# Four conv layers on one core: another order of work in the tap stages, and the gate's chunks spread into them

## The chip, the cores and the metric

The kernel runs on one core of one Trainium2 chip. The metric is the device time of one execution in microseconds (us). Three executions of the kernel before took 1805.18, 1809.2 and 1817.68 us; their median, 1809.2 us, is the time that the change is held against.

## The reference, cut to what matters

The input `x` is (4, 256, 56, 56) in fp32: four images of 256 channels. Four layers follow one another, each with a group norm `_gn` (32 groups) ahead of it and its result added to its input:

```python
# layers 0 and 2: a 7x7 "involution": the taps differ at every pixel, and 16 channels share them
h    = reduce_w @ x            # 256 -> 64 channels (layer 2: then batch norm and relu)
kern = span_w @ h + span_b     # 49 taps for each of 16 groups, at each pixel
out  = sum over the 49 taps of kern * shifted x      # layer 2: then batch norm and relu
# layer 1: two 3x3 convolutions with batch norms and relus
# layer 3: a gate by Fourier transforms
cf = sigmoid(fft2(x).real.mean over pixels @ W.T + b)   # a number for each channel
sf = fft2(x.mean over channels).real                    # a number for each pixel
out = x * cf + x * sf
```

In each layer `x = x + layer(_gn(x))`. The mean over pixels of the transform's real part is the first pixel of `x`, so `cf` needs one small matrix product.

## The kernel before, in words

**Tiling and stages.** `involution_layer` (L280) is called for layer 0 and for layer 2; a convolution layer lies between. It works through eight units, (image b, channel block cb of 128 channels), cb=0 and then cb=1 of each image. A unit has two stages. In its *tap stage*, `tap_matrices` (L569) runs over 32 groups n: TensorE computes the taps of one group (L580) into a pair of PSUM banks, of which there are four pairs, and the pair is evicted with the bias added into the tile `kt`, by ScalarE (six ACTIVATEs, L591) where n % 3 is 0, and by VectorE (one TENSOR_TENSOR, L598) else. In its *column stage*, seven strips of eight pixel columns (tx 0 to 6) are done one after another by `apply`: TensorE multiplies windows of the image `xw` with `kt` (L622), ScalarE and VectorE scale, fold and add the result to the image block `xs` (L635 to L649), and `next_windows` makes the `xw` of a later strip: transposes on TensorE, a copy on ScalarE, and four transfers on SyncE's queue that shift rows (L414, L416).

**What sets the order.** It is written out by hand. `in_order` (L228) keeps every engine's instructions in the order of the program, so an instruction that waits holds all that stand behind it on its engine. Other work is cut into steps (Python generators): `place(hooks, steps, (2, 6, ...))` puts one step each behind those groups n of the tap stage, and the lists `early[tx]` and `late[tx]` put steps before or behind a strip of the column stage.

**Steps in layer 2's hooks.** Layer 3's gate is fused into layer 2. When a unit's image block is done, the next unit's tap stage takes its norm for layer 3: `norm_of(3, ...)`, made of `norm_steps` (L199): a mean over channels by TensorE (L207), differences on VectorE (L215), a second mean (L218), then 1/sqrt(variance), whose power is the GpSimd instruction L139 (hook 12), and the shift on VectorE, L222 (hook 13). In the second and third unit a second norm runs in the tap stage too, that of the last image for layer 2. `channel_mean` (L677) takes the mean over channels on TensorE (L702), and `gate_factors` (L720) loads W (`w3_sb`, SyncE), computes `cf` (L732, L739) and the transforms that give `sf`; this is once per image, in the tap stage of the next image's cb=0. An image's block of 1568 KB is loaded at hook 26 or 21.

**The gate.** For all images but the last, the gate is applied chunk by chunk (`gate_chunk`, L777), on GpSimd alone: 14 chunks per image, seven groups of eight rows by two channel blocks, chunk k being rows k // 2 and channel block k % 2. Each has two steps. `next_load` (every second time with a load of sfb, the row group's `sf` for all partitions, L783) loads the chunk `gx` (L786) into one of three buffers; `next_gate` computes (L789, L794, L795, L796) and stores it (L797). GpSimd starts these transfers itself. They stand in cb=0's column stage (tx 2 to 6), in cb=1's tap stage (hooks 16, 22, 28) and in cb=1's column stage (tx 0 to 5). In that last stage `bottleneck` (L421) makes the next image's `hp`: GpSimd clears a part (L432) at tx 0, ScalarE writes the rest (L478).

The last image's gate is done at the end by other code on more engines, from the last norm on (its power is L139 too).

Of the kernel before, what the change touches and what calls it, by code (L numbers as in the profile page):

```python
# [16 lines left out]
P = 128  # L17
# [54 lines left out]
def net_kernel(  # L72
# [207 lines left out]
    def involution_layer(layer, xin, xout, red, span, sb, xs_of, ahead=None, pending=None):  # L280

        with ExitStack() as es:
# [23 lines left out]
            if layer == 0:  # L306
                load(0, 0, (2, 2, 2, 1))
                load(0, 1, (2, 2, 2, 1))

                nc.scalar.copy(norm_sb[:, 3, B - 1, 1, :], mhalf)  # L310

            red_sb = wpool.tile([P, NB, 2, R], F32, name="red_sb")

# [255 lines left out]
            def tap_matrices(b, cb, hooks):  # L569

                hp = h_of[b]
                kt = big.tile([Q, GB, TP // PB, NT, PB], F32, name="kt")
                for n in range(GB // 2 * TP // PB):
                    gp, pb = divmod(n, TP // PB)
                    ps = two_banks()
                    for k in range(PB):
                        py, px = divmod(pb * PB + k, TX)
                        z0 = ZF - py * QX - px
                        for i in range(2):
                            nc.tensor.matmul(  # L580
                                ps[:Q, i, k * NT : (k + 1) * NT],
                                z_sb[i * R : (i + 1) * R, cb * GB // 2 + gp, z0 : z0 + Q],
                                hp[i * R : (i + 1) * R, py, px].rearrange("p a t -> p (a t)"),
                                start=True,
                                stop=True,
                            )
                    g0, p0 = 2 * gp, pb * PB
                    if n % 3 == 0:
                        for i in range(2):
                            for k in range(PB):  # L590
                                nc.scalar.activation(  # L591
                                    kt[:, g0 + i, pb, :, k],
                                    ps[:Q, i, k * NT : (k + 1) * NT],
                                    AF.Identity,
                                    bias=zb_sb[:, cb * GB + g0 + i, p0 + k : p0 + k + 1],
                                )
                    else:
                        nc.vector.tensor_tensor(  # L598
                            kt[:, g0 : g0 + 2, pb],
                            ps[:Q, :, : PB * NT].rearrange("q i (k t) -> q i t k", k=PB),  # L600
                            zb_sb[:, cb * GB + g0 : cb * GB + g0 + 2, p0 : p0 + PB]
                            .unsqueeze(2)
                            .to_broadcast([Q, 2, NT, PB]),
                            ALU.add,
                        )
                    for h in hooks.get(n, ()):
                        h()
                return kt
# [68 lines left out]
            def channel_mean(b, cb):  # L677
# [39 lines left out]
                nc.sync.dma_start(m2_of[cb], m_dram[b][cb].rearrange("j (r w) -> (j r) w", w=W))  # L717
                yield

            def gate_factors(b):  # L720


                w3_sb = [dead(b, 1, 4 * CR * W + ci * C, C) for ci in range(NB)]
                for ci in range(NB):
                    nc.sync.dma_start(w3_sb[ci], w3[ci * P : (ci + 1) * P])
                cf = small.tile([P, NB], F32, name="cf")
                cf_of[b] = cf
                yield
                for co in range(NB):
                    ps = one_bank()  # L730
                    for ci in range(NB):
                        nc.tensor.matmul(  # L732
                            ps[:, 0:1],
                            w3_sb[ci][:, co * P : (co + 1) * P],
                            first_of[b][:, ci : ci + 1],
                            start=(ci == 0),
                            stop=(ci == NB - 1),
                        )
                    nc.scalar.activation(  # L739
                        cf[:, co : co + 1], ps[:, 0:1], AF.Sigmoid, bias=cp[:, co, L3_B : L3_B + 1]  # L740
                    )
                yield

                ps = one_bank()
                for i in range(2):
                    at = slice(i * R, i * R + W)
                    for cb in range(NB):
                        nc.tensor.matmul(
                            ps[at, :H],
                            m2_of[cb],  # L750
                            sin_sb if i else cs2_sb[:H],
                            start=(cb == 0),
                            stop=(cb == NB - 1),
                        )
                yield
                for i in range(2):
                    at = slice(i * R, i * R + W)
                    nc.vector.tensor_copy(half[at], ps[at, :H])
                yield

                ps = one_bank()
                nc.tensor.matmul(ps[:H, :W], half, cs2_sb, start=True, stop=True)
                scale = small.tile([P, NB], F32, name="gscale")
                bias = small.tile([P, NB], F32, name="gbias")
                nc.vector.tensor_mul(scale, cf, norms[3][b][0])
                nc.vector.tensor_scalar_add(scale, scale, 1.0)
                nc.vector.tensor_mul(bias, cf, norms[3][b][1])
                gate_of[b] = scale, bias
                yield
                sf = small.tile([H, W], F32, name="sf", bufs=1)  # L770
                nc.vector.tensor_copy(sf, ps[:H, :W])
                nc.sync.dma_start(sf_dram[b].rearrange("j (r w) -> (j r) w", w=W), sf)
                yield

            sf_of, gate_of = {}, {}

            def gate_chunk(b, j, cb):  # L777

                rstd, shift = norms[3][b]
                at = slice(j * CR * W, (j + 1) * CR * W)  # L780
                if cb == 0:
                    sf_of[b] = work.tile([P, CR * W], F32, name="sfb", bufs=2)
                    nc.gpsimd.dma_start(sf_of[b], sf_dram[b][j : j + 1].to_broadcast([P, CR * W]))  # L783
                sf = sf_of[b]
                xs = gx_tile()
                nc.gpsimd.dma_start(xs, xout[b][cb][:, at])  # L786
                yield
                xn = work.tile([P, CR * W], F32, name="gn", bufs=1)
                nc.gpsimd.tensor_scalar(  # L789
                    xn, xs, rstd[:, cb : cb + 1], shift[:, cb : cb + 1], ALU.mult, ALU.add  # L790
                )

                scale, bias = (t[:, cb : cb + 1] for t in gate_of[b])
                nc.gpsimd.tensor_scalar(xs, xs, scale, bias, ALU.mult, ALU.add)  # L794
                nc.gpsimd.tensor_tensor(xn, xn, sf, ALU.mult)  # L795
                nc.gpsimd.tensor_tensor(xs, xs, xn, ALU.add)  # L796
                nc.gpsimd.dma_start(ov[b, cb][:, at], xs)  # L797
                yield

# [193 lines left out]
            for u, (b, cb) in enumerate(units):  # L993
                hooks = hooks0 if u == 0 else {}
                if prev is not None:
# [2 lines left out]
                    place(hooks, norm_of(layer + 1, pb, pc, st), (2, 6, 7, 11, 12, 13))  # L998
                    if layer == 2 and u < 3:
                        g = norm_of(2, B - 1, u - 1, pending[1][u - 1])  # L1000
                        place(hooks, g, (19, 20, 22, 23, 25, 26))
                    if layer == 2:
                        place(hooks, channel_mean(pb, pc), (13, 17))
                        if pc == 1:
                            place(hooks, gate_factors(pb), (17, 24, 27, 28, 30, 31))
                        elif pb == B - 1:
                            factors = gate_factors(pb)
                            place(hooks, factors, (20,))
                            hooks.setdefault(21, []).append(lambda pb=pb: last_dft(pb))
                            hooks.setdefault(22, []).append(last_ones)  # L1010
                            place(hooks, first_half(pb), (28, 29))
                    if layer == 2 and cb == 1 and b > 0:
                        for n in (16, 22, 28):
                            hooks.setdefault(n, []).extend((next_gate, next_load))
                if b + 1 < B:
                    n = 16 if layer == 0 else (26, 21)[cb]
                    hooks.setdefault(n, []).append(load_step(b + 1, cb))
# [42 lines left out]
                        early[6].append(step(g))  # L1060
                if layer == 2 and b > 0:
                    if cb == 0:
                        chunks.extend(gate_chunk(b - 1, j, c) for j in range(NCHUNK) for c in range(NB))
                        late[1] += [next_load, next_load]
                    for tx in range(2, NTX) if cb == 0 else range(NTX - 1):
                        late[tx] += [next_gate, next_load]
                if last_image and cb == 0:
                    for tx in range(6):
                        late[tx] += [step(g2)] * 3
# [652 lines left out]
```

## Time and profile before

| | us |
|---|---|
| median of three executions | 1809.2 |
| the profiled execution, of which all durations here come | 1812.46 |
| its span, first to last instruction | 1810.7 |
| layer 0 | 38 to 476 |
| convolution layer | 510 to 1240 |
| layer 2 with the gate | 1240 to 1811 |
| a tap stage, layer 0 | 24.8 to 28.2 each |
| a tap stage, layer 2 | 28.7 to 36.1 each |
| a column stage, layer 2 | 28.3 to 36.2 each |
| idle of TensorE in one stage, layer 2 | up to 5.4 |

The granted TensorE clock was 0.979 of full speed. In the profile's lines PE is TensorE's matmul, PEld its weight load, DVE VectorE, ACT ScalarE, POOL GpSimd and SP SyncE; L12 is line 12 of the kernel before. A row `PE ps L580 <- ACT kt L591: 5.8, 15, 0.9` says that TensorE's instructions of L580 waited 5.8 us in all, 15 times, 0.9 at the longest, for ScalarE's writes of `kt`, the eviction that frees a PSUM pair. A timeline's line has the start in us from the span's start, the duration, engine, line, operation, tile written and tiles read, and in brackets the wait before it with what ended it.

### The profile page before, as it was taken

How to read it: one execution, taken by the hardware profiler on the slowest of the kernel's cores; microseconds unless marked ns; L12 is line 12 of the kernel's file. 1: busy time of each engine (PE TensorE's matmuls, PEld its weight loads, DVE VectorE, ACT ScalarE, POOL GpSimd, SP SyncE). 2: the span in 40 equal slices, each digit the busy share in tenths (PEclk: the TensorE clock that was granted, in tenths of full speed). 3: DMA queues.
4: the chain of work that ended last, by engine and by line, in shares of the span. 5: the costliest groups of instructions: out<-in, count | busy, mean ns of one | idle time of the engine just before them, and what ended most of it. 6: DMA issues, size and time to landing. Idle time of an engine off the chain costs nothing.

```text
span 1810.7 us, 55835 instructions
## 1 busy us (share of the span) xinstructions
PE 1720.8 (95%) x24034; PEld 1514.9 (84%) x24034; DVE 1375.4 (76%) x2729; ACT 842.2 (47%) x1981; POOL 430.0 (24%) x626
## 2 busy tenths in 40 slices
PE   7999999999989999999999999997999999899988
PEld 6998989889878988998899889985988887887876
DVE  3787777776689988898889888875777677677775
ACT  3566556555532322322232222113767567577564
POOL 2333433245210000000000000000000374563572
PEclk9999999999989999999999999998999999999997
DMA  2545534454651201120121111031534566665653
GB/s 85 158 154 165 164 119 143 159 159 116 209 174 49 69 26 63 63 70 30 59 73 59 41 60 34 34 135 49 161 132 149 168 218 188 202 210 168 169 156 127
DMA packets 66004, 215.77 MB, mean 119 GB/s; under 512 B 13237, under 2 KB 20926, under 8 KB 62046
## 3 DMA queue, kind: packets, MB, share of 16 engines
q1 hardware_dynamic: 48718, 145.24, 25.7%
q0 software_dynamic: 14688, 64.78, 11.3%
q8 instruction: 190, 3.11, 0.7%
q10 hardware_dynamic: 2352, 2.18, 0.4%
q14 instruction: 56, 0.46, 0.1%
HBM read 76.30 MB, written 49.15 MB: 69 GB/s over the span
## 4 chain that ended last, share of the span: by engine, by line
PE 76%; DVE 9%; ACT 6%; DMA 4%; issue 2%; POOL 2%; SPq 1%; ACTq 0%; POOLq 0%; DVEq 0%
PE mm L1493 19%; PE ps L580 18%; PE ps L622 14%; PE mm L1411 10%; PE mm L1382 5%; PE ps L396 5%; DMA xw<-xw 4%; ACT kt L591 3%; PE ps L459 2%; DVE un L642 1%; DVE kt L598 1%; ACT xw L408 1%; ACT hp L478 1%; SPq L414 1%; DVE res L1486 1%
## 5 line engine op out<-in xcount | busy, mean ns | idle before, releaser
L580 PE MATMUL ps<-hp,z_sb 64*126 64x133 f32 x6144 | 392.1, 281 | 16.2 <-ACT kt L591 7.0
L622 PE MATMUL ps<-kt,xw 126*32 126x48 f32 (+1 forms) x12544 | 379.0, 236 | 24.1 <-DMA xw<-xw 12.1
L622 PEld LDWEIGHTS ps<-kt,xw 126*32 126x32 f32 (+1 forms) x12544 | 341.9, 122 | 68.2 <-issue 46.3
L580 PEld LDWEIGHTS ps<-hp,z_sb 64*126 64x126 f32 x6144 | 369.1, 187 | 34.6 <-ACT kt L591 12.7
L598 DVE TENSOR_TENSOR kt<-ps,zb_sb 126x798 f32<-126x798 f32 x336 | 319.8, 981 | 90.1 <-PE ps L580 89.5
L1493 PE MATMUL mm<-v,u_sb 128*128 128x280 f32 (+1 forms) x1728 | 385.0, 385 | 3.4 <-DVE v L1318 3.4
L1493 PEld LDWEIGHTS mm<-v,u_sb 128*128 128x128 f32 x1728 | 327.9, 190 | 57.5 <-DVE v L1318 3.8
L591 ACT ACTIVATE kt<-ps,zb_sb 126x133 f32<-126x133 f32 x1056 | 306.9, 442 | 96.2 <-PE ps L580 95.6
L1411 PE MATMUL mm<-v,u_sb 128*128 128x252 f32 (+1 forms) x936 | 212.3, 388 | 3.4 <-DVE v L1302 3.4
L1411 PEld LDWEIGHTS mm<-v,u_sb 128*128 128x128 f32 x936 | 178.3, 192 | 33.8 <-issue 3.5
L1530 POOL DMA_DIRECT2D x<-xs x24 | 13.1, 546 | 683.2 <-DVE xs L1529 427.4
L642 DVE SCALAR_TENSOR_TENSOR un<-ps,s,un 128x240 f32<-128x240 f32 x224 | 102.5, 457 | 85.7 <-ACT un L637 81.5
L642 DVE SCALAR_TENSOR_TENSOR un<-ps,par_sb,un 128x240 f32<-128x240 f32 x224 | 98.3, 457 | 87.1 <-ACT un L635 82.8
L1478 ACT ACTIVATE res<-xs,shift,norm_sb 128x1120 f32<-128x1120 f32 (+1 forms) x24 | 30.2, 1259 | 236.3 <-DVE xs L1529 107.3
L408 ACT COPY xw<-ps 126x896 f32<-126x896 f32 x112 | 101.4, 906 | 47.9 <-PE ps L396 37.7
L647 POOL TENSOR_TENSOR xs<-un,xs 128x240 f32<-128x240 f32 x112 | 72.3, 664 | 192.4 <-DVE un L642 192.3
L396 PE MATMUL ps<-ident_sb,strip_sb 128*126 128x128 f32 x784 | 111.7, 283 | 6.1 <-POOL strip_sb L381 5.8
L635 ACT ACTIVATE un<-ps,par_sb 128x240 f32<-128x240 f32 x112 | 50.1, 448 | 115.7 <-PE ps L622 113.4
L1382 PE MATMUL mm<-xs,u_sb 128*128 128x126 f32 (+1 forms) x792 | 98.6, 277 | 1.3 <-DVE xs L1345 0.9
L396 PEld LDWEIGHTS ps<-ident_sb,strip_sb 128*126 128x126 f32 x784 | 84.9, 142 | 17.0 <-POOL strip_sb L381 6.9
L637 ACT ACTIVATE un<-ps,bn_t,s 128x240 f32<-128x240 f32 x112 | 60.0, 538 | 83.3 <-PE ps L622 72.1
L1382 PEld LDWEIGHTS mm<-xs,u_sb 128*128 128x128 f32 x792 | 94.5, 191 | 2.4 <-issue 1.0
(254 smaller groups left out, 1925.8 us busy)
## 6 DMA issues: line engine op xcount, KB each, us to landing
xw<-xw SPq DMA_DIRECT2D x168, 252.0 KB
xw<-xw SPq DMA_DIRECT2D x224, 126.0 KB
xw<-xw POOLq DMA_DIRECT2D x56, 252.0 KB, 4.7
xs<-x SPq DMA_DIRECT2D x24, 560.0 KB
x<-xs POOLq DMA_DIRECT2D x8, 1568.0 KB, 8.2
xs<-x SPq DMA_DIRECT2D x8, 1568.0 KB
xs<-in_x_dram SPq DMA_DIRECT2D x6, 1568.0 KB
x<-xs SPq DMA_DIRECT2D x6, 1568.0 KB
```

Of the source, the lines that this page charges most:

```text
L396: nc.tensor.transpose(ps[:Q, k * P : (k + 1) * P], flat[:, k * Q : (k + 1) * Q], ident_sb)
L408: nc.scalar.copy(xw[:, :NSB, :], ps[:Q, : NSB * P].rearrange("q (n c) -> q n c", n=NSB))
L580: nc.tensor.matmul(ps[:Q, i, k * NT : (k + 1) * NT], z_sb[i * R : (i + 1) * R, cb * GB // 2 + gp, z0 : z0 + Q], hp[i * R : (i + 1) * R, py ...
L591: nc.scalar.activation(kt[:, g0 + i, pb, :, k], ps[:Q, i, k * NT : (k + 1) * NT], AF.Identity, bias=zb_sb[:, cb * GB + g0 + i, p0 + k : p0 ...
L598: nc.vector.tensor_tensor(kt[:, g0 : g0 + 2, pb], ps[:Q, :, : PB * NT].rearrange("q i (k t) -> q i t k", k=PB), zb_sb[:, cb * GB + g0 : cb ...
L622: nc.tensor.matmul(v[m * j : m * j + m, i, :, k * TP : (k + 1) * TP], xw[:, window(ty), m * j : m * j + m], kt[:, ng * j : ng * j + ng, :, ...
L637: nc.scalar.activation(part, o[0], AF.Identity, bias=bn["t4"][:, cb : cb + 1], scale=bn["s4"][ng][:, 0, cb : cb + 1])
L642: nc.vector.scalar_tensor_tensor(part, o[e], s, part, ALU.mult, ALU.add)
L647: nc.gpsimd.tensor_tensor(dst, u, dst, ALU.add)
L1382: nc.tensor.matmul(ps[:, co * m : (co + 1) * m], u[ci][:, co * P : (co + 1) * P], v2[:, e, : n // 2, ci * WT : (ci + 1) * WT], start=(ci = ...
L1411: nc.tensor.matmul(ps, u1_sb[:, ci, dy, k, co * P : (co + 1) * P], v[:, k, dy * NB + ci : (dy + n - 1) * NB + ci + 1 : NB, :], start=(j == 0),
L1493: nc.tensor.matmul(ps, u2_sb[:, ci, dy, k, co * P : (co + 1) * P], v[:, k, dy * NB + ci : (dy + n - 1) * NB + ci + 1 : NB, :], start=(j == 0),
```

## The change

In words, in the order of the diff:

- The first copy on ScalarE, which fills a value of the table of norms, is an activation with the function Sigmoid.
- ScalarE evicts the groups with n % 3 equal to 2, so 10 of 32 in place of 11; the first two and the last two groups are VectorE's. This holds for both involution layers.
- `w3_sb` goes into buffers of sfb for all images but the last, and its load is issued at hook 8 in place of 17.
- The gate's two numbers per channel are others: cf + 1/rstd, and −shift/rstd. A chunk is computed as gn = x·rstd + shift, then (sf + cf + 1/rstd)·gn − shift/rstd, which equals x + (cf + sf)·gn: three TENSOR_SCALAR and one TENSOR_TENSOR in place of two and two.
- sfb's first two loads stand at cb=0's tx 0; each other one is issued in a gate of cb=1's chunks, before that gate's store, two row groups ahead.
- The two first chunks of gx are loaded in cb=0's tap stage, at hooks 18 and 20. From then on each place has a load and then a gate, in place of a gate and then a load.
- The places of gates: cb=0's columns tx 1, 2, 4, 5; cb=1's tap stage, hooks 14, 18, 22, 26, 30; cb=1's columns tx 0 to 4.
- The second norm's steps stand at hooks 15, 19, 20, 24, 25, 26 in place of 19, 20, 22, 23, 25, 26.

```diff
-                nc.scalar.copy(norm_sb[:, 3, B - 1, 1, :], mhalf)
+                nc.scalar.activation(norm_sb[:, 3, B - 1, 1, :], mhalf, AF.Sigmoid)
...
-                    if n % 3 == 0:
+                    if n % 3 == 2:
...
+            def new_sf():
+                return work.tile([P, CR * W], F32, name="sfb", bufs=2)
+
             def gate_factors(b):
-                w3_sb = [dead(b, 1, 4 * CR * W + ci * C, C) for ci in range(NB)]
+                w3_sb = [new_sf()[:, :C] if b < B - 1 else dead(b, 1, 4 * CR * W + ci * C, C) for ci in range(NB)]
...
-                nc.vector.tensor_mul(scale, cf, norms[3][b][0])
-                nc.vector.tensor_scalar_add(scale, scale, 1.0)
-                nc.vector.tensor_mul(bias, cf, norms[3][b][1])
-                gate_of[b] = scale, bias
+                rstd, shift = norms[3][b]
+                nc.vector.reciprocal(back, rstd)
+                nc.vector.tensor_add(cfx, cf, back)
+                nc.vector.scalar_tensor_tensor(back, shift, -1.0, back, ALU.mult, ALU.mult)
+                gate_of[b] = cfx, back
...
+            def load_sf(b, j):
+                sf_of[b, j] = new_sf()
+                nc.gpsimd.dma_start(sf_of[b, j], sf_dram[b][j : j + 1].to_broadcast([P, CR * W]))
+
             def gate_chunk(b, j, cb):
-                if cb == 0:
-                    sf_of[b] = work.tile([P, CR * W], F32, name="sfb", bufs=2)
-                    nc.gpsimd.dma_start(sf_of[b], sf_dram[b][j : j + 1].to_broadcast([P, CR * W]))
-                sf = sf_of[b]
                 xs = gx_tile()
                 nc.gpsimd.dma_start(xs, xout[b][cb][:, at])
                 yield
...
-                nc.gpsimd.tensor_scalar(xs, xs, scale, bias, ALU.mult, ALU.add)
-                nc.gpsimd.tensor_tensor(xn, xn, sf, ALU.mult)
-                nc.gpsimd.tensor_tensor(xs, xs, xn, ALU.add)
+                nc.gpsimd.tensor_scalar(xs, sf_of[b, j], 1.0, cfx, ALU.mult, ALU.add)
+                nc.gpsimd.tensor_tensor(xs, xs, xn, ALU.mult)
+                nc.gpsimd.tensor_scalar(xs, xs, 1.0, back, ALU.mult, ALU.add)
+                if cb == 1 and j + 2 < NCHUNK:
+                    load_sf(b, j + 2)
                 nc.gpsimd.dma_start(ov[b, cb][:, at], xs)
...
-                        place(hooks, g, (19, 20, 22, 23, 25, 26))
+                        place(hooks, g, (15, 19, 20, 24, 25, 26))
...
-                            place(hooks, gate_factors(pb), (17, 24, 27, 28, 30, 31))
+                            place(hooks, gate_factors(pb), (8, 24, 27, 28, 30, 31))
+                            chunks.extend(gate_chunk(pb, j, c) for j in range(NCHUNK) for c in range(NB))
+                            for n in (18, 20):
+                                hooks.setdefault(n, []).append(next_load)
...
-                        for n in (16, 22, 28):
-                            hooks.setdefault(n, []).extend((next_gate, next_load))
+                        for n in (14, 18, 22, 26, 30):
+                            hooks.setdefault(n, []).extend((next_load, next_gate))
...
                     if cb == 0:
-                        chunks.extend(gate_chunk(b - 1, j, c) for j in range(NCHUNK) for c in range(NB))
-                        late[1] += [next_load, next_load]
-                    for tx in range(2, NTX) if cb == 0 else range(NTX - 1):
-                        late[tx] += [next_gate, next_load]
+                        late[0] += [lambda b=b, j=j: load_sf(b - 1, j) for j in range(2)]
+                    for tx in (1, 2, 4, 5) if cb == 0 else range(NTX - 2):
+                        late[tx] += [next_load, next_gate]
```

More of the change, by code (lines that the diff above doesn't have):

```diff
@@ L762, in gate_factors @@
                 nc.tensor.matmul(ps[:H, :W], half, cs2_sb, start=True, stop=True)
-                scale = small.tile([P, NB], F32, name="gscale")
-                bias = small.tile([P, NB], F32, name="gbias")
-                nc.vector.tensor_mul(scale, cf, norms[3][b][0])
-                nc.vector.tensor_scalar_add(scale, scale, 1.0)
-                nc.vector.tensor_mul(bias, cf, norms[3][b][1])
-                gate_of[b] = scale, bias
+                cfx = small.tile([P, NB], F32, name="gscale")
+                back = small.tile([P, NB], F32, name="gbias")
+                rstd, shift = norms[3][b]
[3 more added lines that the diff above has]
+                gate_of[b] = cfx, back
                 yield
@@ L791, in gate_chunk @@
                 )
[L793 to L796, printed above, removed]
+                cfx, back = (t[:, cb : cb + 1] for t in gate_of[b])
+                nc.gpsimd.tensor_scalar(xs, sf_of[b, j], 1.0, cfx, ALU.mult, ALU.add)
[3 more added lines that the diff above has]
+                    load_sf(b, j + 2)
                 nc.gpsimd.dma_start(ov[b, cb][:, at], xs)
```

## The prediction

> **What bounds the kernel now.** I read the engines' totals, then each engine's waits in the second involution layer (1130 to 1811 us, where most of the diff lies), then GpSimd's timeline and its transfers.
>
> ```profile
> PE 1720.8 (95%) x24034; PEld 1514.9 (84%) x24034; DVE 1375.4 (76%) x2729; ACT 842.2 (47%) x1981; POOL 430.0 (24%) x626
> ```
>
> TensorE has work for 95% of the span, so only about 90 us of idle can be won, and anything that holds it up is paid in full. Its waits by releaser (total us, count, longest), and below them GpSimd's:
>
> ```profile
> PE ps L622 <- DMA xw<-xw: 10.6, 10, 3.8
> PE ps L580 <- ACT kt L591: 5.8, 15, 0.9
> PE ps L702 <- DVE kt L598: 2.8, 3, 1.0
> PE ps L218 <- DVE d L215: 2.3, 2, 1.1
> PE ps L207 <- DVE mv L204: 1.9, 2, 0.9
> PE ps L732 <- ACT kt L591: 1.8, 1, 1.8
> ```
> ```profile
> POOL norm_sb L139 <- DVE norm_sb L138: 202.6, 10, 84.4
> POOL gn L789 <- DMA gx<-x: 18.1, 16, 3.9
> POOL gx L786 <- DMA out_dram<-gx: 6.4, 6, 2.2
> ```
>
> TensorE's waits are many and small; five of these six rows are touched. GpSimd waits most for the norm's power (L139): it comes there early. For a finished store (last row) it waits only 6.4 us, since a chunk's buffer is one of three and was stored a whole gate earlier. GpSimd's timeline (start, duration, wait before it in brackets) shows a gate, and one of those waits:
>
> ```profile
> 1443.37 0.71 POOL L789 TENSOR_SCALAR gn<-gx,norm_sb 128x448 f32<-128x448 f32 x1 [0.34 <-DMA gx<-x]
> 1444.18 0.71 POOL L794 TENSOR_SCALAR gx<-gx,gscale,gbias 128x448 f32<-128x448 f32 x1
> 1444.86 1.14 POOL L795 TENSOR_TENSOR gn<-gn,sfb 128x448 f32<-128x448 f32 x1
> 1446.08 1.14 POOL L796 TENSOR_TENSOR gx<-gx,gn 128x448 f32<-128x448 f32 x1
> 1447.52 0.59 POOL L797 DMA_DIRECT2D out_dram<-gx  x1 [0.30 <-POOL gx L796]
> 1448.11 0.55 POOL L783 DMA_DIRECT2D sfb<-sf  x1
> 1448.65 0.55 POOL L786 DMA_DIRECT2D gx<-x  x1
> ...
> 1482.71 0.55 POOL L786 DMA_DIRECT2D gx<-x  x1 [2.23 <-DMA out_dram<-gx]
> 1483.25 0.17 POOL L432 MEMSET hp<- 128x56 f32 x1
> ```
>
> The stores' line answers how long one takes from issue to landing:
>
> ```profile
> L797 POOL DMA_DIRECT2D out_dram<-gx x42: 592/592/619, 1435.9 to 1780.4; - x42
> DMA to landing us min/median/max: 2.3/4.7/8.4
> ```
>
> **What the Trainium skill says.** (1) "DMA: Bandwidth & Descriptors", "Anatomy of one DMA — SWDGE (gpsimd) path": a transfer started by GpSimd has a fixed part of about 2.0 us besides its bytes. The trace agrees: a 224 KB store never lands in under 2.3 us. (2) The same page, "Issuing engines are not separate DMA queues": all starters' transfers "interleave with each other". The trace agrees: stores land in 2.3 us in quiet stretches, 3.3 to 3.9 in lightly loaded columns, 7 to 8 beside a 1568 KB image. (3) "SBUF — State Buffer", "Who interferes with whom": VectorE's second port pair is GpSimd's, under an exclusive lock. The trace agrees in part: VectorE's L649 grows from 0.41 us to 0.78 to 1.07 beside gates, while the kt eviction L598, which reads PSUM, keeps 0.98.
>
> **The change, part by part.**
>
> *Gates, order and buffers.* A step is now load, gate in place of gate, load. So the load of chunk k+2 comes before gate k, and its buffer, of three, is that of chunk k−1, whose store is the instruction just before on GpSimd. Every such load therefore waits a store's whole landing, L. Queued behind it on GpSimd are the gate, then the norm's power L139 (behind it VectorE's shift L222, then kt evictions in program order, then TensorE), and the memset L432 (ACT's L478 waits for it).
>
> One gate costs GpSimd, without waits: 4.15 us from L789's start to the store's issue (1447.52 − 1443.37). The changed arithmetic has three TENSOR_SCALAR and one TENSOR_TENSOR in place of two and two: −(1.14 − 0.71) = −0.43, so 3.72. With a load at 0.57 and half an sfb load (0.55/2 = 0.27), the pitch is 4.56 + L, against 5.65 to 5.9 measured now.
>
> Between the power in a cb=1 tap stage and that in the next cb=0 tap stage lie 10 gates, 8 loads of which 7 wait, 3 sfb loads, 3 last store issues and the memset: 37.2 + 4.6 + 1.65 + 1.8 + 0.2 = 45.4, plus 7L. These powers stand 65.4 us apart in the first image (1463.97 to 1529.34) and 64.9 in the second. GpSimd keeps up while L is below (65.4 − 45.4)/7 = 2.9, or 2.8. The third image's next power is the tail's, which is already close:
>
> ```profile
> 1785.61 0.57 POOL L139 TENSOR_TENSOR norm_sb<-norm_sb,mhalf 128x1 f32<-128x1 f32 x1 [4.63 <-DVE norm_sb L138]
> ```
>
> It comes 57.5 us after the one at 1728.15. There 45.2 + 7L must fit into 57.5, plus 2.2 of TensorE work that runs behind it anyway: L below 2.1.
>
> What L will be, no row shows: loads no longer overlap the stores, but the column stages' xw transfers and the images stay. The bounds are 2.3 (the fastest store) and 4.9 (the mean of 42). I take 4.0, between the lightly loaded columns and the median, and 3.6 for the last image, which has no image load beside it. Then 45.4 + 28 = 73.4: the powers come **8.0** and **8.5** late, and the tail's 45.2 + 25.2 − 57.5 − 2.2 = **10.7**. Sum **+27.2**. At 2.3 it is 0 + 0 + 1.6; at 4.9, 14.3 + 14.8 + 19.8 = 49. The memset, behind gates 4 to 8, comes at 23.4 + 4L = 39 after the power; ACT's first L478 ran 31.8 after it. That is a delay of the same 8 us, not a second one. The four gates in cb=0 columns end some 4 us before the power; nothing is lost there. The cheaper arithmetic is hidden as long as GpSimd keeps up, and is inside the 3.72 otherwise.
>
> *Second norm's hooks* (units 1 and 2). The groups between its steps grow, so L207 (0.94), L218 (1.14) and the L580 after each (0.48, 0.86) no longer wait, in either unit: the rows sum to 4.2 for the first two over two units; with L580, 4.2 + 2 × 1.34 = 6.9. I take **−5.0** (bounds −4.2 and −6.9).
>
> *w3's load* at hook 8 in place of 17, into sfb's buffers: the L732 waits (1.8 in the row, 0.93 before another releaser) go: **−2.8**. On SyncE it now stands behind the previous image's last gate; next in that queue are transfers of hooks 17 and later, so nothing is late. VectorE's three small operations stay three: 0.
>
> *Two gx loads of each image leave the cb=0 columns for hooks 18 and 20, and two gates leave columns* (5, 3 and 6 gates in cb=0 columns, cb=1 taps and cb=1 columns become 4, 5 and 5). xw's waits there were 1.07 + 1.38, 3.77 and 0.42 + 1.73 = 8.4; the transfers that remain still share the engines, so I take half, **−4** (bounds 0 and −8.4).
>
> *n % 3 == 2.* ACT has 10 groups of 1.75 us in place of 11, VectorE 22 of 0.98 in place of 21. Two VectorE groups now start and end each stage; the column stage waits for the last of them. I take 0.4 in three gate units and 0.1 in 13 others: 1.2 + 1.3. Group 7, which carries a norm step, waits for VectorE's group 4, 0.17 in four stages of the first layer: 0.7. In the second layer the start's wait, which looks like this,
>
> ```profile
> 1321.60 2.32 PE L580 MATMUL ps<-hp,z_sb 64*126 64x133 f32 x36 [0.64 <-ACT kt L591]
> ```
>
> goes, and about as much appears at group 7. Sum **+3.2** (bounds −5.8, if nothing replaces that row, and +8).
>
> *Sigmoid at the start.* One table load of 1.28 us goes at 1411.39, where ACT then sat idle till 1415.57: 0 (bounds 0 and −1.3).
>
> *Sum.* 27.2 − 5.0 − 2.8 − 4 + 3.2 = **+18.6**. The profiled execution took 1812.46 us (span 1810.7, 1.76 around it), so 1831 for it; it lies 3.3 above the shown runs' median of 1809.2, and the forecast in terms of that is **1828**.
>
> **Rivals.** *A, the forecast:* GpSimd's landings set powers and tail, L from 3.3 to 4.7: slope 7 us per image and us of L, 1814 to 1842; 0.56. For it: the buffer's arithmetic, and a median landing of 4.7. Against: the longest landings stood beside transfers that now move. *B, on the other side:* with gx's load held back, a store meets less traffic and lands in about 2.6; GpSimd keeps up with both powers and only the tail is 45.2 + 18.2 − 59.7 = 3.7 late. Then −8.6 + 3.7 = −4.9: **1804**. It decides at L = 3.0, where two images' 1.0 and 1.5 and the tail's 6.5 just eat the 8.6. For it: quiet stores of 2.3. Against: sfb's load is issued just before half of the stores. 0.20. *C:* landings as in B, xw's waits gone altogether (−4.4 more), the L580 row not replaced (−5.8 in place of +3.2), and half of L702's 2.8 saved: −4.9 − 4.4 − 9 − 1.4, about **1789**; 0.10. *D:* stores land in 4.9 or more, as now or worse: 49 − 8.6 = +40, **1849**; 0.14. *VectorE as the bound in tap stages* is no case of its own: 22 × 0.93 (its pitch) = 20.5 us, and some 4 of hooks, against 24.8 of TensorE.
>
> **How the numbers follow.** About 1%, 18 us, is what a measurement of this kernel can tell from no change. Faster by more (below 1791) needs C or the best of B: 0.11. Within: the rest of B and the lower half of A: 0.43. Slower (above 1827): A's upper half and D: 0.46. The range leaves out most of C and D's upper part: 1796 to 1846.
>
> **What would show it.** Right: the gx load's wait for out_dram<-gx grows from 6.4 us to over 100 in all, gates stand 8 to 9 us apart, L139 follows a gate at once in place of waiting for L138, L222 waits for L139, ACT's L478 for hp, and the tail's power is some 10 us late against the tail's start. L207's, L218's and L732's waits are gone; there is one table load. Wrong: gates at under 7.5 us, so that L139 still waits for VectorE (B); or new waits of the xw transfers, which I have not priced.

## The result, and the profile after

The changed kernel took 1839.9 us (median of 4 runs, 1835.56 to 1844.05) beside 1813.44 us for the kernel before (4 runs): a ratio of 1.0132, 95% interval 1.0101 to 1.0162. It is slower, by 18 to 29 us; 1828 was forecast, with a range of 1796 to 1846. As a difference, +18.6 us was forecast (against a median of 1809.2) and some +24 measured, by the ratio. Its profiled execution took 1840.69 us, 28.2 above that of the kernel before.

The engines' totals of the changed kernel, then TensorE's waits in its second involution layer and GpSimd's from 1395 us on, where the gates begin (total us, count, longest):

```profile
PE 1718.6 (93%) x24034; PEld 1509.9 (82%) x24034; DVE 1385.3 (75%) x2745; ACT 816.4 (44%) x1884; POOL 404.7 (22%) x626
```
```profile
PE ps L702 <- DVE mean L694: 29.9, 2, 16.4
PE ps L878 <- POOL norm_sb L139: 14.2, 1, 14.2
...
PE ps L580 <- DVE kt L598: 4.4, 10, 0.5
PE ps L622 <- DMA xw<-xw: 4.2, 6, 1.1
...
PE ps L580 <- ACT kt L591: 0.9, 2, 0.6
```
```profile
POOL norm_sb L139 <- DVE norm_sb L138: 66.1, 5, 47.8
POOL gx L790 <- DMA out_dram<-gx: 117.8, 32, 6.0
```

TensorE has the work that it had (1718.6 us busy against 1720.8), so the loss is all waiting: 44.1 us lie in three waits (29.9 in two, 14.2 in one). The granted clock was 0.970 here and 0.979 before, but TensorE's busy time has not grown, so the loss does not lie there. All small rows that the prediction showed have shrunk or are gone: L207 and L218 no longer wait, and L732 (L735 here) waits 0.3 us. On GpSimd the load of gx (L790 here, L786 before) waits 117.8 us for stores, where it waited 6.4, and the power L139 waits 66.1 us for VectorE, where it waited 103.3 from 1395 us on.

How the load's wait reaches TensorE shows in three timelines of one place, GpSimd's, VectorE's and TensorE's (`issue` in a bracket: nothing that the profile shows ended the wait):

```profile
1517.74 0.54 POOL L790 DMA_DIRECT2D gx<-x  x1 [3.66 <-DMA out_dram<-gx]
1518.32 0.72 POOL L793 TENSOR_SCALAR gn<-gx,norm_sb 128x448 f32<-128x448 f32 x1
...
1522.04 0.59 POOL L803 DMA_DIRECT2D out_dram<-gx  x1 [0.30 <-POOL gx L800]
1528.82 0.54 POOL L790 DMA_DIRECT2D gx<-x  x1 [6.18 <-issue]
...
1541.84 0.59 POOL L803 DMA_DIRECT2D out_dram<-gx  x1 [0.30 <-POOL gx L800]
1542.45 0.57 POOL L139 TENSOR_TENSOR norm_sb<-norm_sb,mhalf 128x1 f32<-128x1 f32 x1
```
```profile
1543.06 0.16 DVE L222 SCALAR_TENSOR_TENSOR norm_sb<-gm,norm_sb 128x1 f32<-128x1 f32 x1 [17.15 <-POOL norm_sb L139]
...
1543.45 0.38 DVE L694 TENSOR_SCALAR mean<-cmean,norm_sb 128x32 f32<-128x32 f32 x2
```
```profile
1543.97 0.29 PE L702 MATMUL ps<-one,mean 128*32 128x1 f32 x8 [16.38 <-DVE mean L694]
```

The power L139 has no wait in brackets: it runs the moment the last gate's store is issued, 1541.84 + 0.61. In the kernel before it waited 8.92 us for VectorE at this place:

```profile
1529.34 0.56 POOL L139 TENSOR_TENSOR norm_sb<-norm_sb,mhalf 128x1 f32<-128x1 f32 x1 [8.92 <-DVE norm_sb L138]
```

VectorE's shift (L222) has been waiting for 17.15 us, with the small operations that make `mean` and the evictions queued behind it, and TensorE for 16.38. The chain of work that ended last names the same: the stores' landings are 8% of it, and GpSimd is 10% where it was 2%.

The stores' line answers as follows:

```profile
L803 POOL DMA_DIRECT2D out_dram<-gx x42: 544/595/607, 1429.5 to 1815.8; - x42
...
DMA to landing us min/median/max: 2.3/3.8/6.3
```

The median landing fell from 4.7 to 3.8 us. The stores land sooner now that the loads of gx are held back, but most of them are waited for.

### The profile page after: what moved, and what is told of

Read it like the earlier page. It is cut to its first block, busy times and chain, and to the rows that moved or that the text cites. A ratio compares the mean times of both kernels' runs of the same rounds, so it can differ in the third digit from the quotient of the medians.

```text
span 1838.9 us, 55766 instructions
## 1 busy us (share of the span) xinstructions
PE 1718.6 (93%) x24034; PEld 1509.9 (82%) x24034; DVE 1385.3 (75%) x2745; ACT 816.4 (44%) x1884; POOL 404.7 (22%) x626
## 4 chain that ended last, share of the span: by engine, by line
PE 60%; DVE 12%; POOL 10%; DMA 9%; issue 5%; ACT 3%; SPq 0%; POOLq 0%; ACTq 0%; DVEq 0%
PE mm L1501 18%; PE ps L580 10%; PE mm L1419 10%; PE ps L622 9%; DMA out_dram<-gx 8%; PE mm L1390 5%; DVE kt L598 4%; POOL gx L799 3%; PE ps L396 3%; DVE un L642 2%; POOL gn L793 2%; POOL gx L798 2%; POOL gx L800 1%; PE ps L459 1%; DVE res L1494 1%
## 5 line engine op out<-in xcount | busy, mean ns | idle before, releaser
L580 PE MATMUL ps<-hp,z_sb 64*126 64x133 f32 x6144 | 385.6, 279 | 14.0 <-DVE kt L598 5.7
L580 PEld LDWEIGHTS ps<-hp,z_sb 64*126 64x126 f32 x6144 | 365.2, 186 | 31.9 <-issue 8.7
L598 DVE TENSOR_TENSOR kt<-ps,zb_sb 126x798 f32<-126x798 f32 x352 | 333.0, 980 | 63.8 <-PE ps L580 63.2
L591 ACT ACTIVATE kt<-ps,zb_sb 126x133 f32<-126x133 f32 x960 | 280.7, 442 | 111.6 <-PE ps L580 111.4
L1486 ACT ACTIVATE res<-xs,shift,norm_sb 128x1120 f32<-128x1120 f32 (+1 forms) x24 | 30.2, 1258 | 237.0 <-DVE xs L1537 107.2
L408 ACT COPY xw<-ps 126x896 f32<-126x896 f32 x112 | 101.6, 907 | 45.6 <-PE ps L396 36.1
L647 POOL TENSOR_TENSOR xs<-un,xs 128x240 f32<-128x240 f32 x112 | 72.2, 666 | 191.6 <-DVE un L642 191.4
```

The lines of the kernel that those rows point to most:

```text
L408: nc.scalar.copy(xw[:, :NSB, :], ps[:Q, : NSB * P].rearrange("q (n c) -> q n c", n=NSB))
L580: nc.tensor.matmul(ps[:Q, i, k * NT : (k + 1) * NT], z_sb[i * R : (i + 1) * R, cb * GB // 2 + gp, z0 : z0 + Q], hp[i * R : (i + 1) * R, py ...
L591: nc.scalar.activation(kt[:, g0 + i, pb, :, k], ps[:Q, i, k * NT : (k + 1) * NT], AF.Identity, bias=zb_sb[:, cb * GB + g0 + i, p0 + k : p0 ...
L598: nc.vector.tensor_tensor(kt[:, g0 : g0 + 2, pb], ps[:Q, :, : PB * NT].rearrange("q i (k t) -> q i t k", k=PB), zb_sb[:, cb * GB + g0 : cb ...
L647: nc.gpsimd.tensor_tensor(dst, u, dst, ALU.add)
```

## The experiments

Ratios are to the kernel before, run beside the experiment on the same chip; 0.001 is 1.8 us. Two theories were held against each other first. *The queue:* the load's wait for the store just issued delays the norm's power behind it. *The place:* the gates in the tap stages cost by being there, whatever their order.

### The order alone, undone in the changed kernel

```diff
-                        for n in (14, 18, 22, 26, 30):
-                            hooks.setdefault(n, []).extend((next_load, next_gate))
+                            hooks.setdefault(n, []).extend((next_gate, next_load))
...
-                        late[tx] += [next_load, next_gate]
+                        late[tx] += [next_gate, next_load]
```

> The changed kernel with one thing undone: in each place the gate stands before the load again, so a load meets a buffer that was stored a whole gate earlier. Theory (the load's wait for the store just issued delays the norm's power): that wait falls from 117.8 us to under 15 us in all, gates stand under 6.3 us apart, TensorE's waits of 29.9 us (L702) and 14.2 us (L878) go, and the gains stay: 1840 less about 43 us, 1797 (1790 to 1806), a ratio to the kernel before of about 0.991. Rival (gates in the tap stages cost by their own traffic or their place, whatever order they have with loads): above 1825, a ratio over 1.006.

Measured: 1797.95 us, ratio 0.9893 (0.9875 to 0.9911). GpSimd's waits from 1390 us on, and TensorE's:

```profile
POOL norm_sb L139 <- DVE norm_sb L138: 124.4, 8, 47.7
...
POOL gn L793 <- DMA gx<-x: 11.1, 11, 1.7
POOL gx L790 <- DMA out_dram<-gx: 9.5, 7, 3.4
```
```profile
PE ps L622 <- DMA xw<-xw: 9.5, 10, 2.3
```

L702 and L878 are gone from TensorE's waits, and GpSimd waits for VectorE again. The same gates in the same places, some 43 us faster (1.0132 − 0.9893 of 1813): the place is not the cause, the order is. This is also a version that beats both kernels. But xw's waits are back at 9.5 us, where the changed kernel has 4.2 and the kernel before 10.6. These are single profiles: the same row reads 9.6, 9.1 and 5.4 in the three single gains below, which leave the gates as they were before. A difference of 5 us in it is therefore not clear of chance.

### The wait kept, the power taken out of its queue

```diff
-        rsqrt_eps(rstd, ps[:, 0:1], GN_EPS)
+        if layer == 3:
+            nc.vector.tensor_scalar_add(rstd, ps[:, 0:1], GN_EPS)
+            nc.vector.reciprocal(rstd, rstd)
+        else:
+            rsqrt_eps(rstd, ps[:, 0:1], GN_EPS)
...
-                w3_sb = [new_sf()[:, :C] if b < B - 1 else dead(b, 1, 4 * CR * W + ci * C, C) for ci in range(NB)]
+                w3_sb = [dead(b, 1, 4 * CR * W + ci * C, C) for ci in range(NB)]
...
-                            place(hooks, gate_factors(pb), (8, 24, 27, 28, 30, 31))
+                            place(hooks, gate_factors(pb), (17, 24, 27, 28, 30, 31))
```

> The changed kernel with all its waits for stores kept, but with the norm of layer 3 taken off GpSimd: its power is replaced by a reciprocal on VectorE, so the square root of the variance is left out and the output is another; w3's load is back at hook 17 and in its old place, so that it doesn't wait for a gate either. Theory (the store's wait costs only because the power is queued behind it): the load's wait stays at 90 to 130 us in all, but L702's 29.9 us and L878's 14.2 us go, and the time is 1797 to 1810, a ratio of about 0.995; the end is bounded by the last gates, which then end at about 1800. Rival (late gates cost in other ways: traffic beside the columns, the memset of hp, which then comes late for the next tap stage): above 1822, with new waits of L580 for the memset L432 or of L622 for xw.

Measured: 1805.73 us, ratio 0.9935 (0.9907 to 0.9964). In this kernel the load of gx is L794, and the square root of the norm is left out. GpSimd's wait for stores is longer than ever, and ScalarE's timeline near the end shows what is left of its cost:

```profile
POOL gx L794 <- DMA out_dram<-gx: 131.6, 32, 7.3
```
```profile
1778.08 0.76 ACT L834 ACTIVATE gx<-xs,norm_sb 128x448 f32<-128x448 f32 x1 [13.43 <-DMA out_dram<-gx]
1782.27 0.76 ACT L834 ACTIVATE gx<-xs,norm_sb 128x448 f32<-128x448 f32 x1 [3.42 <-DMA out_dram<-gx]
1782.93 0.39 ACT L746 ACTIVATE cf<-ps,cp 128x1 f32<-128x1 f32 x2
```

With 131.6 us of waiting in place, some 36 us of the changed kernel's time are gone (1.0132 − 0.9935 of 1813): the wait costs only through what is queued behind it. At the end the last image's norm needs the three gx buffers, the last gates hold them, and `cf` stands behind on ScalarE; TensorE waits 7.1 us there. So the gates do bound the end of this kernel, as expected.

### The order alone, in the kernel before

```diff
-                            hooks.setdefault(n, []).extend((next_gate, next_load))
+                            hooks.setdefault(n, []).extend((next_load, next_gate))
...
-                        late[tx] += [next_gate, next_load]
+                        late[tx] += [next_load, next_gate]
```

> The kernel before with one thing changed: load and then gate, in place of gate and then load, in the same places. From the power in a cb=1 tap stage to the next there are then 9 gates of 4.15, 7 loads of 0.57, 3 sfb loads of 0.55 and 6 waits for a landing of 4.4 plus 0.3: about 72 us, against 65.4 and 64.9. Theory: the powers of the first two images come some 7 us late each and the tail's some 10 us, together +18 to +30 us, a ratio of 1.010 to 1.017, with a load's wait of 70 to 110 us in all. Rival (the order alone is harmless, what hurts is that the changed kernel has two more gates behind the power): within 6 us, 0.998 to 1.004.

Measured: 1860.47 us, ratio 1.0229 (1.0202 to 1.0256): more than was expected. Two powers of this kernel, the one in the second gate image's cb=1 tap stage and the tail's:

```profile
1625.81 0.57 POOL L139 TENSOR_TENSOR norm_sb<-norm_sb,mhalf 128x1 f32<-128x1 f32 x1
...
1838.76 0.57 POOL L139 TENSOR_TENSOR norm_sb<-norm_sb,mhalf 128x1 f32<-128x1 f32 x1
```

Neither waits for VectorE. I had counted three late powers, those that close a stretch of gates over cb=1. In fact the three in cb=1's tap stages are late too: five gates with landings no longer fit between the transform's result and the power, whereas the change has four gates there, with the first two loads done ahead. TensorE's L702 waited 34.1 us in five places, and 6.7 more came at the tail; xw's waits rose from 10.6 to 15.8. The order does by itself what the theory said; the size was short by the powers left out.

### Fewer of the waits

```diff
-                            hooks.setdefault(n, []).extend((next_load, next_gate))
+                            hooks.setdefault(n, []).extend((next_gate, next_load))
```

In the changed kernel, in cb=1's tap stage only.

> The changed kernel with gate and then load in cb=1's tap stage only; both column stages keep load and then gate. Of the 7 loads behind each power that waited for a whole landing, 3 are left (the ones in cb=1's columns). Theory (a threshold: GpSimd's work and waits between two powers cost nothing until they fill the 64 us between them): the chain is 45.4 + 3 x 4.4 and some 3 us of waits for gx, 61 to 62 us, against 63.7 and 64.5 us; the powers of images 1 and 2 are not late and the tail's by at most 2 us: 1795 to 1801, a ratio of 0.988 to 0.992, though the load's waits are still 70 to 90 us in all. Rival (a cost per wait: the 21 waits cost 46 us, 2.2 us each, so the 9 that are left cost 20): a ratio of 0.999 or more.

Measured: 1812.11 us, ratio 0.9973 (0.9958 to 0.9988): between the two expectations. The waits answer why:

```profile
POOL gx L790 <- DMA out_dram<-gx: 88.1, 20, 7.7
```
```profile
PE ps L702 <- DVE mean L694: 7.4, 2, 3.7
...
PE ps L878 <- POOL norm_sb L139: 2.3, 1, 2.3
```

In the first two stretches the waits were longer than the 3 × 4.4 us and 3 us that I had put in. For each stretch from a power in cb=1's tap stage to the next, the table sets the loads' waits beside the length; the last column is the stretch in the first experiment, where VectorE and not GpSimd ends it.

| stretch | changed: length, waits, rest | this kernel: length, waits, rest | first experiment |
|---|---|---|---|
| first image | 80.4, 30.2, 50.2 | 68.7, 19.0, 49.7 | 63.7 |
| second | 78.0, 28.1, 49.9 | 68.0, 18.4, 49.6 | 64.5 |
| third, to the tail | 72.2, 22.3, 49.9 | 61.5, 11.9, 49.6 | 55.2 |

The rest is the same in all six, 49.6 to 50.2 us: that is GpSimd's own work with its small gaps, and the stretch is that plus the waits. So some 14 us of waiting are free in each of the first two stretches and 5 in the third. Waits of 19.0 then cost 5.0 (68.7 − 63.7), waits of 30.2 cost 16.7. That is a threshold and no cost per wait (30.2 is 1.6 times 19.0, its cost 3.3 times). This kernel's three delays, 5.0, 3.5 and 6.3, sum to 14.8 us, and its ratio is 14.5 us above the first experiment's. So the expected time was missed in two ways: the waits of the first two stretches were longer than I put in, and the third chain, though 61.5 us long as expected, ran against a stretch of only 55.2.

### The single gains

Each of the next three is the kernel before with one part of the change.

```diff
-                    if n % 3 == 0:
+                    if n % 3 == 2:
```

> The kernel before with ScalarE's evictions at n % 3 equal to 2 alone, in both involution layers. As forecast: +3.2 us, ratio 1.0018 (0.2 to 1.0 us more idle of TensorE at the end of tap stages, a wait for VectorE's group 4 in place of the start's wait). Rival (VectorE is near its limit in the gate units, and 22 groups make it the bound there): +8 us or more, 1.0045 and above. Rival (the 5.8 us of L580's waits for ScalarE go and nothing takes their place): -3 us or less, below 0.9985.

Measured: ratio 0.9993 (0.9978 to 1.0008). The forecast's 1.0018 lies outside; there is no loss and no gain that can be told. Of L580's 5.8 us of waits for ScalarE 0.9 were left, and its waits for VectorE rose from 1.7 to 4.9.

```diff
-                        place(hooks, g, (19, 20, 22, 23, 25, 26))
+                        place(hooks, g, (15, 19, 20, 24, 25, 26))
```

> The kernel before with the second norm's six hooks moved alone. As forecast: -5 us (-4.2 to -6.9), a ratio of 0.9972, with L207's 1.9 and L218's 2.3 us gone and nothing in their place. Rival (the tap stages of units 1 and 2 became 3.2 and 5.0 us shorter in the changed kernel, and all of it is this part's): -8 us, 0.9955. Rival (the wait moves to another step of the norm): within 1.5 us.

Measured: ratio 0.9976 (0.9962 to 0.9989), 4.4 us, as forecast. L207 and L218 left TensorE's waits, and the two tap stages shrank from 31.8 and 36.1 to 29.5 and 33.0 us.

```diff
+            def new_sf():
+                return work.tile([P, CR * W], F32, name="sfb", bufs=2)
...
-                w3_sb = [dead(b, 1, 4 * CR * W + ci * C, C) for ci in range(NB)]
+                w3_sb = [new_sf()[:, :C] if b < B - 1 else dead(b, 1, 4 * CR * W + ci * C, C) for ci in range(NB)]
...
-                            place(hooks, gate_factors(pb), (17, 24, 27, 28, 30, 31))
+                            place(hooks, gate_factors(pb), (8, 24, 27, 28, 30, 31))
```

> The kernel before with w3 in buffers of sfb and its load at hook 8 in place of 17, alone. As forecast: L732's waits (1.8 and 0.9 us) go, -2.8 us, a ratio of 0.9985. Rival (the load on SyncE stands behind the last gate's reading of sfb, and the transfers of channel_mean's hook 17 behind it are late): 0 or slower, above 0.9995, with L732 or the matmuls of the transforms waiting in its place.

Measured: ratio 0.9976 (0.9960 to 0.9992). The forecast's 0.9985 lies inside; L732's waits are gone.

The next two start from the first experiment, all gates first.

```diff
-                            for n in (18, 20):
-                                hooks.setdefault(n, []).append(next_load)
...
-                        for n in (14, 18, 22, 26, 30):
+                        for n in (16, 22, 28):
...
                         late[0] += [lambda b=b, j=j: load_sf(b - 1, j) for j in range(2)]
+                        late[1] += [next_load, next_load]
-                    for tx in (1, 2, 4, 5) if cb == 0 else range(NTX - 2):
+                    for tx in range(2, NTX) if cb == 0 else range(NTX - 1):
```

> All gates first, and the gates and first loads of gx back in the places that the kernel before has (5, 3 and 6 gates; no loads of gx at hooks 18 and 20); arithmetic, sfb's loads, w3, evictions and the second norm as changed. As forecast, moving them is worth 4 us by fewer waits of xw: 1802, a ratio of 0.991 to 0.993. Rival (it is worth nothing, since with all gates first xw's waits were 9.5 us beside 10.6 before): as the all-gates-first kernel, 0.988 to 0.990.

Measured: 1801.06 us, ratio 0.9923 (0.9901 to 0.9945). That is what 4 us from the places would give, but the interval meets the first experiment's (0.9875 to 0.9911), and xw's waits, which were to carry it, are 7.0 us here against 9.5 there, lower and not higher. So the places may be worth something, but nothing shows that they are worth it by xw; how is open.

```diff
-                nc.gpsimd.tensor_scalar(xs, sf_of[b, j], 1.0, cfx, ALU.mult, ALU.add)
-                nc.gpsimd.tensor_tensor(xs, xs, xn, ALU.mult)
-                nc.gpsimd.tensor_scalar(xs, xs, 1.0, back, ALU.mult, ALU.add)
+                nc.gpsimd.tensor_scalar(xs, xs, cfx, back, ALU.mult, ALU.add)
+                nc.gpsimd.tensor_tensor(xn, xn, sf_of[b, j], ALU.mult)
+                nc.gpsimd.tensor_tensor(xs, xs, xn, ALU.add)
```

(and the two numbers per channel as the kernel before makes them.)

> All gates first, as in the first experiment, and the gate's arithmetic of the kernel before (two operations of 0.71 and two of 1.14 us in place of three and one; the two numbers per channel by mul, add, mul again). As forecast the cheaper arithmetic is hidden as long as GpSimd keeps up: a ratio as the first experiment's 0.989 (0.987 to 0.991), and L139 still waits for VectorE. Rival (the second operation with two SBUF inputs holds VectorE's small operations up, so that L702 waits again): 0.992 to 0.994, with 2 us or more of L702 in TensorE's waits.

Measured: 1805.94 us, ratio 0.9942 (0.9923 to 0.9962), its interval apart from the first experiment's. VectorE's timeline behind the first gate's power, with the old arithmetic and then with the new (first experiment):

```profile
1461.38 1.72 DVE L694 TENSOR_SCALAR mean<-cmean,norm_sb 128x32 f32<-128x32 f32 x2
```
```profile
1460.47 0.67 DVE L694 TENSOR_SCALAR mean<-cmean,norm_sb 128x32 f32<-128x32 f32 x2
```

The pair of L694 starts 1.50 us after the power in one and 1.52 in the other, and takes 1.72 against 0.67 us (and 0.38 in the changed kernel, shown above, where GpSimd only issues transfers at that moment). GpSimd's operation with two SBUF inputs starts 2.05 and 2.10 us after the power; with the old arithmetic the pair ends at 1463.10, just when that operation does (1463.06). With the old arithmetic L702 waits 2.7 us in three places again, with the new not at all. This fits the Trainium skill, "SBUF — State Buffer", "Who interferes with whom": an exclusive lock on the ports that VectorE and GpSimd share, where the one that issues first holds up the other. That a few hundredths of a microsecond decide here is my reading of these two timelines and was not tested by itself. Over the layer L694 takes 6.6 us in all with the old arithmetic and 3.5 with the new, and VectorE's addition L649 57.1 and 52.4. L702's waits account for 2.7 of some 9 us; the rest lies in small amounts over tap and column stages and is not settled.

### Load first only where the power is not behind

All gates first behind the power, but load and then gate in cb=0's column stage, to keep the changed kernel's short waits for xw:

```diff
-                        late[tx] += [next_load, next_gate]
+                        late[tx] += [next_load, next_gate] if cb == 0 else [next_gate, next_load]
```

(and gate, load in cb=1's tap stage.)

> The changed kernel with gate and then load behind the power (cb=1's tap and column stages), but load and then gate, as the change has it, in cb=0's column stage, where the four gates end ahead of the power anyway. Theory (the order costs only where the power stands close behind; and in cb=0's columns it holds gx's load back from xw's transfers, which is where TensorE lost 2.9, 4.9 and 5.2 us with all gates first, against 1.5, 1.7 and 1.3 in the changed kernel): some 8 us below the all-gates-first kernel's 1798, 1790 (1785 to 1795), a ratio of 0.985. Rival (those stalls were low in the changed kernel only because everything stood later against the images' transfers): 1798, 0.989, with xw's waits at 9 us as there. Rival (four loads behind stores make the power of the cb=1 tap stage late): above 1800, with waits of L222 for L139.

Measured: 1794.98 us, ratio 0.9885 (0.9862 to 0.9908), the lowest of all but not to be told from the first experiment's 0.9893. TensorE's idle in the three cb=0 column stages was 3.2, 2.4 and 1.4 us, 7.0 against 12.9 there, but the cb=1 column stages idled about 2 us more, and xw's waits came to 7.2 in all. The 8 us that I expected did not come.

## Why the prediction was right

**The mechanism** was right at every link of the chain to TensorE: the buffer stored by the instruction just before, the wait for a whole landing, the power behind it, L222 and the evictions behind that, TensorE last. Undoing the order removed the loss, adding the order to the kernel before produced one, and taking the power out of the queue disarmed the wait. A side branch, through the memset L432, was wrong (see the smaller steps).

**The landing** L, which no row showed, was put at 4.0 us and 3.6 for the last image. The seven stores waited for in each stretch landed in 4.04, 4.08 and 3.43 us on average.

**The delays** were nevertheless too small. Forecast were 8.0, 8.5 and 10.7 us. Against the first experiment, TensorE's idle in the two tap stages is 17.9 to 1.0 and 15.1 to 1.3 us, and the tail is 47.9 to 32.8 us long: delays of 16.9, 13.8 and 15.1. The chains were 80.4, 78.0 and 72.2 us long, not 73.4, 73.4 and 70.4. Three terms were missing:

- From a landing to the load's start there are 0.28 us, 2.0 per stretch.
- The first load behind each power waited too, 1.45, 1.70 and 0.56 us; I had counted it as the one that does not wait.
- One load of the first stretch started 3.2 us after its store's landing (the 6.18 us above). No cause is shown, but it is no accident of this run: in all twelve profiles GpSimd's 127th transfer of the execution starts after such a pause, of 3.18 or 3.19 us where it need not wait for a store as well. The profile before has it too, where GpSimd had time to spare:

```profile
1509.20 0.59 POOL L797 DMA_DIRECT2D out_dram<-gx  x1 [3.18 <-issue]
```

The powers would also have come sooner than I took them, 63.7, 64.5 and 55.2 us apart and not 65.4, 64.9 and 57.5, since the gains shorten the stretch that the chain must fit into: 4.4 us in all.

**The gains** were mis-sized as well, −8.6 net against some −19 (ratio 0.9893). The second norm (−5.0; 4.4 measured) and w3 (−2.8; 4.4 measured, 1.5 to 7.3) fit. The evictions were put at +3.2, and the interval around 0.9993 excludes that. The cheaper arithmetic was put at 0 because GpSimd's own time is hidden; it is worth some 9 us. In part it works, as the timelines suggest, through VectorE's operations, whose shared ports I had cited and not priced; the larger part is open. The −4 for xw is not shown: with all gates first its waits were 9.5 us, and with the old places 7.0.

So that 1828 came near 1840 is in part luck: two sums, +27 and −9, were both too small by far, and the errors cancel. About +46 (43 by the ratios) and −19 stand in their place.

**Smaller steps.** I said that ScalarE's first L478 waits for the memset L432, and counted its delay as part of the first 8 us. It does not wait: L478 ran at 1499.58 and 1503.33, the memset at 1504.82. The second table load is gone, as forecast, and worth nothing visible. w3's load did wait on SyncE for the previous image's last gate (40.5 us in all, 13.2 at the longest), and TensorE's L735 waited only 0.3 us.

**The rivals.** B needed an L under 3.0, and it was 4.0. The first experiment, where hardly a load waits for a landing, ends on B's side (0.9893), and further than B's 1804. D's cost came nearly true (49 us forecast, 46 measured) without D's cause, landings of 4.9.

## What to carry to other kernels

When buffers go round, count how many instructions lie between a buffer's store and its next load on the issuing engine: swapping two steps can take that from a whole step to none. Then find what is queued behind the wait, and compare the chain of work and waits with the time between two uses: here 14 us of waiting were free in two stretches and 5 in the third, and what went beyond was paid in full on another engine. A forecast of such a chain needs the restart after a landing as well as the landing and the pauses that the profile before already shows, and must be made against the stretch as the other parts of the change leave it.

## What the runs showed that I had not expected

- Two small VectorE operations took 0.38 us while GpSimd only issued transfers, 0.67 beside the new arithmetic and 1.72 beside the old, whose operation with two SBUF inputs began 0.05 us sooner after the power; and one change of arithmetic on a mostly idle GpSimd moved the kernel by 0.5% (0.9893 to 0.9942).
- Holding the loads back shortened the stores' landings (median 4.7 to 3.8 us, and 4.7 to 3.1 where only the order was changed); letting them run again brought 4.8 back.
- GpSimd's 127th transfer started after a pause of some 3.2 us in the profile of every kernel, whether it was a load or a store.
